# Quantizing tokens and down weights among the scans instead of ahead of them, in a fused state-space and FP4 feed-forward block

## The chip, the cores and the metric

The kernel runs on one core of one Trainium2 chip. The metric is device time in microseconds (us): the median over runs of the whole program. The core has five engines that work side by side, each through its own instructions in order: TensorE (PE; its weight loads are listed as PEld), VectorE (DVE), ScalarE (ACT), GpSimd (POOL) and SyncE (SP), which here issues nearly all transfers between the device's main memory and the on-chip memory (SBUF). Matrix products land in a second on-chip memory, PSUM, which PE, DVE and ACT reach. Engines wait for each other through semaphores.

## What is computed

Input is x of 8 x 1024 tokens of 512 features; the output is x plus two branches that both read the layer-normalized tokens. In short:

```python
xn = (x - mean(x)) / sqrt(var(x) + 1e-5)
# branch 1: selective state-space layer, 1024 inner channels, 16 states
xb, z = split(xn @ W_in)                     # 512 -> 2 x 1024
xc = silu(causal_conv4(xb) + conv_b)
B, C, d = split(xc @ W_x)                    # 16, 16 and 1 column
dt = softplus(d + dt_bias)
h_t = h_{t-1} * exp(dt_t * A) + dt_t * xc_t * B_t      # per channel and state
y = (sum_states(h_t * C_t) + xc * D) * silu(z)
out1 = y @ W_out
# branch 2: feed-forward with FP4 blocks of 16, 1408 inner features
def fp4(v):                                  # per block of 16 along the last axis
    s = max(max(abs(v)) / 6, 1e-12)
    return nearest_of(0, .5, 1, 1.5, 2, 3, 4, 6)(abs(v / s)) * sign(v) * s
g = fp4(xn) @ fp4(w_gate).T;  u = fp4(xn) @ fp4(w_up).T
out2 = fp4(silu(g) * u) @ fp4(w_down).T
out = x + out1 + out2
```

## The kernel before

The 8192 tokens are cut into 16 steps of 512 (two to a sequence); a step is four tiles of 128 tokens. The recurrence runs along time in one DVE instruction, the scan (`scan`, L553). A scan covers 128 rows (32 channels by 4 states) and two stretches of 512 time steps, so 64 scans, called pairs here, make a step, and there are 1,024.

**A pair.** POOL makes `u` (`make_u`, L523, two pairs ahead, three buffers), ACT makes the decays `ah` in PSUM with two exponentials (`make_a`, L535, one pair ahead, two buffers), DVE scans `ah` with `u` and multiplies by C into `hc` (L560, four buffers), PE sums the states into `py` (`sum_states`, L570).

**The preparation.** All that the pairs and the feed-forward read is made first and left in main memory (`run`, L795 to L815): gate and up weights in 12 pieces (`prepare_gate_up`), down weights in 8 (`prepare_down`), tokens in 32 halves of a step (`normalize`). Each piece is quantized (`quantize`: the maximum of each block of 16 at L74, scales, the product with the inverse scale at L81, all on DVE; `step_of`, ACT's absolute value and exponential, which give the rounding step; POOL's sum, difference and product at L83 to L85), then transposed on PE and copied by ACT (`transposed`). A token half is transposed twice, normalized alone (`xnT`, for branch 1) and quantized (`xqT`, for branch 2). Its pool has two buffers of each tile. Step 0's projections and convolution (`ahead`) are woven in, one part after each piece.

**The pairs' stage.** The order is written out by hand (`tc.manual_schedule`), pair by pair, in `sweep`: `make_u`, `make_a`, `scan`, then what fell due (`issue`), then other work by a budget of time per pair. Other work comes from generators that yield their estimated cost: `finish` (the step before: output projection, pairs 2 to 9), `ahead` (the next step: projections, convolution with ACT's `taps` and POOL's sums at L365, from pair 9 on), and `others`: in steps 0 to 9 `gate_up` (gate and up products, silu, quantization of the hidden piece on DVE, ACT and POOL at L671 to L693, transposes L706), in steps 10 to 15 `downs` (L779). `later(n, work)` puts work n pairs ahead; a work that returns `AGAIN` is put off by a pair; `key` keeps an order, and `act` limits ACT's long work in a pair. PE's products outside `py` take one of three PSUM banks (`bank`, `frees`), and a generator is only asked while `room` finds one. After step 9's last pair `gate_up` is run to its end before `downs` starts.

## Time and profile before

| | us |
|---|---|
| median of 3 runs | 5291.96 (5284.35 to 5296.69) |
| the profiled execution: its time | 5304.77 |
| its span, first to last instruction | 5302.8 |
| first scan starts at | 567.6 |
| steps 0 to 9 | 567.6 to 3716.3 |
| steps 10 to 15, and the last projection | 3716.3 to 5302.8 |
| mean granted clock of PE | 0.90 |

Busy time is the time in which an engine had an instruction in work. A page cuts the span in 40 slices of 132.6 us and shows each engine's busy share in tenths. A table by stretches gives busy us and, in brackets, the instructions; then PE's granted clock, the transfer engines' share and GB/s. A wait is shown as who waited for whom: us in total, how often, the longest. In a group of instructions stand line, engine, operation, out<-in, shapes and count, then busy us and the mean ns of one, then the engine's idle time before them and who ended it.

### The profile page before, as it was taken

What the parts mean: (1) busy time and instruction counts of PE and PEld (TensorE: products, weight loads), DVE (VectorE), ACT (ScalarE), POOL (GpSimd) and SP (SyncE); (2) the same over time, 40 slices, a digit from 0 to 9 for tenths busy, and PEclk for the clock granted to TensorE, in tenths of its full rate; (3) what the DMA queues carried; (4) which work ended last, traced back from release to release, by engine and by line L of the source; (5) the groups of instructions that cost most, each with busy time, mean ns of one, the idle gap of its engine ahead of it and who ended that gap; (6) DMA issues with size and microseconds to landing.
All of it is one profiled execution on the core that took longest, in us unless ns stands there. A gap on an engine that the chain in (4) does not pass through costs nothing.

```text
span 5302.8 us, 52505 instructions
## 1 busy us (share of the span) xinstructions
PE 4385.3 (83%) x16324; PEld 2301.2 (43%) x16324; DVE 4498.5 (85%) x4191; ACT 3408.8 (64%) x5089; POOL 4041.0 (76%) x2338
## 2 busy tenths in 40 slices
PE   4433688989889898988988889896999999999975
PEld 2222446455555645555564555652333333333321
DVE  3477688888888889888897888889898999999997
ACT  4655567685767758676675767767465656665543
POOL 6655688887878889887897888878676777777664
PEclk8655799999999999998999999997999999999986
DMA  5555457565575766656565576756677778687852
GB/s 160 159 159 156 134 155 202 160 196 161 159 197 152 204 174 180 182 163 181 168 191 155 168 187 177 204 144 192 173 219 188 219 187 241 172 240 188 233 132 60
DMA packets 625191, 937.48 MB, mean 177 GB/s; under 512 B 54400, under 2 KB 373888, under 8 KB 622736
## 3 DMA queue, kind: packets, MB, share of 16 engines
q1 hardware_dynamic: 614512, 931.61, 63.1%
q10 hardware_dynamic: 10400, 2.52, 0.2%
q8 instruction: 130, 2.13, 0.2%
q14 instruction: 149, 1.22, 0.1%
HBM read 676.76 MB, written 257.20 MB: 176 GB/s over the span
## 4 chain that ended last, share of the span: by engine, by line
PE 26%; DVE 21%; ACT 12%; DMA 5%; issue 4%; POOL 3%; SPq 0%; DVEq 0%; ACTq 0%; POOLq 0%
DVE ah L553 12%; PE po L620 8%; DVE hc L560 6%; PE pu L656 4%; PE pod L779 4%; ACT ah L535 4%; PE pg L656 3%; PE py L570 2%; PE pz L383 2%; PE px L345 2%; DMA rep<-ddd 2%; POOL u L523 1%; DMA xz<-z 1%; ACT L535 1%; ACT taps L359 1%
## 5 line engine op out<-in xcount | busy, mean ns | idle before, releaser
L523 POOL TENSOR_TENSOR u<-rep,B 128x1024 f32<-128x1024 f32 x1024 | 2409.9, 2359 | 755.0 <-DVE ah L553 695.7
L535 ACT ACTIVATE ah<-rep,A 128x512 f32<-128x512 f32 x2048 | 1415.9, 692 | 1139.1 <-DVE hc L560 1102.5
L560 DVE TENSOR_TENSOR hc<-ah,C 128x1024 f32<-128x1024 f32 x1024 | 1248.6, 1219 | 78.2 <-PE py L570 35.5
L553 DVE TENSOR_TENSOR_SCAN ah<-ah,state,u 128x1024 f32<-128x1024 f32 x512 | 1199.1, 2342 | 89.2 <-ACT u L541 88.2
L553 DVE TENSOR_TENSOR_SCAN ah<-ah,u 128x1024 f32<-128x1024 f32 x512 | 1169.4, 2284 | 65.2 <-ACT ah L535 60.4
L570 PE MATMUL py<-hc,summed 128*32 128x512 f32 x4096 | 648.8, 633 | 170.6 <-DVE hc L560 119.8
L656 PE MATMUL pu<-wu,xq 128*128 128x256 f32 (+1 forms) x3072 | 695.7, 384 | 102.5 <-ACT hT L709 63.5
L656 PE MATMUL pg<-wg,xq 128*128 128x256 f32 (+1 forms) x3072 | 662.6, 373 | 71.0 <-ACT hT L709 27.0
L656 PEld LDWEIGHTS pu<-wu,xq 128*128 128x128 f32 x3072 | 573.1, 203 | 252.5 <-ACT hT L709 88.2
L779 PE MATMUL pod<-dT,hTr 128*128 128x512 f32 x1408 | 645.4, 609 | 17.3 <-DMA hTr<-hT 9.2
L656 PEld LDWEIGHTS pg<-wg,xq 128*128 128x128 f32 x3072 | 555.1, 196 | 211.3 <-issue 70.2
L383 PE MATMUL pz<-xT,wz 128*128 128x512 f32 x1024 | 513.2, 648 | 79.7 <-ACT h L667 34.8
L345 PE MATMUL px<-xT,wx 128*128 128x512 f32 x1024 | 491.1, 624 | 38.1 <-ACT h L667 21.4
L365 POOL TENSOR_TENSOR xc<-xc,taps 128x509 f32<-128x509 f32 (+2 forms) x384 | 440.6, 1147 | 52.9 <-ACT taps L359 34.1
L620 PE MATMUL po<-Wout,y 128*128 128x512 f32 x1024 | 466.7, 608 | 12.4 <-ACT hT L709 4.4
L779 PEld LDWEIGHTS pod<-dT,hTr 128*128 128x128 f32 x1408 | 263.8, 193 | 400.3 <-issue 362.0
L383 PEld LDWEIGHTS pz<-xT,wz 128*128 128x128 f32 x1024 | 206.5, 208 | 354.9 <-issue 235.9
L570 PEld LDWEIGHTS py<-hc,summed 128*32 128x32 f32 x4096 | 91.0, 110 | 561.3 <-DVE hc L560 282.7
L345 PEld LDWEIGHTS px<-xT,wx 128*128 128x128 f32 x1024 | 194.7, 198 | 315.5 <-issue 223.4
L620 PEld LDWEIGHTS po<-Wout,y 128*128 128x128 f32 x1024 | 192.2, 193 | 282.2 <-issue 258.9
L671 DVE TENSOR_TENSOR h<-h,pu 128x512 f32<-128x512 f32 x192 | 121.6, 636 | 190.0 <-PE pu L656 176.6
L535 ACT ACT_TABLE_LOAD x209 | 268.1, 1283 | 3.7
(113 smaller groups left out, 4619.5 us busy)
## 6 DMA issues: line engine op xcount, KB each, us to landing
rep<-ddd SPq DMA_DIRECT2D x512, 512.0 KB, 7.1
ddd<-dd SPq DMA_DIRECT2D x128, 512.0 KB, 4.5
hTr<-hT SPq DMA_DIRECT2D x64, 704.0 KB, 6.7
wg<-gu SPq DMA_DIRECT2D x80, 512.0 KB, 4.9
wu<-gu SPq DMA_DIRECT2D x80, 512.0 KB, 5.2
hT<-hT SPq DMA_DIRECT2D x80, 512.0 KB, 3.1
wx<-in_L_attn_W_in_dram SPq DMA_DIRECT2D x128, 256.0 KB, 3.0
wz<-in_L_attn_W_in_dram SPq DMA_DIRECT2D x128, 256.0 KB, 2.9
```

What stands on the lines that cost most here:

```text
L345: nc.tensor.matmul(px, w[:, k, :], s.xT[:, k, :], start=(k == 0), stop=(k == self.KM - 1))
L365: tt(ca[:, H0 - k :], ca[:, H0 - k :], taps[k][:, : T - H0 + k], ALU.add)
L383: nc.tensor.matmul(b[0], w[:, k, :], s.xT[:, k, :], start=(k == 0), stop=(k == self.KM - 1))
L523: self.nc.gpsimd.tensor_tensor(u, s.reps[j][:, h : h + 2, 1, :], s.B[q].unsqueeze(1).to_broadcast([P, 2, T]), ALU.mult)
L535: nc.scalar.activation(ah[:, i, :], s.reps[j][:, h + i, 0, :], AF.Exp, scale=self.A[:, g, q : q + 1])
L553: nc.vector.tensor_tensor_scan(a, a, u.rearrange("p i t -> p (i t)"), 0.0 if s.first else self.state[:, g, q : q + 1], ALU.mult, ALU.add,)
L560: nc.vector.tensor_tensor(hc, ah, s.C[q].unsqueeze(1).to_broadcast([P, 2, T]), ALU.mult)
L570: nc.tensor.matmul(s.py[i * D4 : (i + 1) * D4, :], self.summed, hcs[i // 2][:, i % 2, :], start=(q == 0), stop=(q == NG - 1),)
L620: nc.tensor.matmul(b[0], s.y[:, j, i * P : (i + 1) * P], self.Wout[:, j, :], start=(j == 0), stop=(j == self.J - 1),)
L656: nc.tensor.matmul(b[0][:, i, :], xq[pair][:, k, i * P : (i + 1) * P], w[:, k, :], start=(k == 0), stop=(k == self.KM - 1),)
L671: nc.vector.tensor_tensor(rows, rows, b[0], ALU.mult)
L779: nc.tensor.matmul(b[0], h[:, k, :], dT[:, k, :], start=(k == 0), stop=(k == self.KF - 1))
```

## The change

The preparation keeps the gate and up weights and the tokens of steps 0 to 2 (`FIRST = 3`). The tokens of the other 13 steps (52 tiles of 128 x 512) and the down weights (12 tiles, four of them 384 columns wide) are handled in the pairs' stage, one tile at a time:

- `measure`: in step 0, a token tile a pair is loaded and DVE takes its mean and variance; `norms` then makes all factors at once.
- `tile_later`: the tile is loaded again; ACT normalizes it in place (`normal`) and PE transposes it (`turn`); DVE takes the block maxima, POOL the two scales (`scale`); DVE the reciprocal, POOL the product (`quotient`); ACT absolute value and exponential, POOL sum, difference and product (`round_`); PE transposes again. ACT copies each transpose, SP stores it. Down tiles have no normalization and one transpose.
- `next_tile` starts a tile when the one before has come far enough, in all of step 0 and in pairs 10 to 52 of the others. `turn_tiles` takes free PSUM banks for transposes and counts 0.5 us of the budget for each. `gate_up` waits with the load of a step's tokens until all four tiles are stored.
- In the preparation `quantize` has its last product on DVE with the scale in PSUM, tokens are stored before they are quantized, step 0's quantization comes after four weight pieces, `ahead` takes two parts after each piece, and step 0's convolution runs on DVE from PSUM (`convolve_first`).
- The tiles `r` of residuals come from one pool with four buffers, shared with the new tiles.

Blank lines and unchanged lines are left out.

```diff
@@ -38,6 +38,7 @@
 AGAIN = "again"
+FIRST = 3
 TAIL = 12
@@ -73,8 +74,6 @@
     nc.vector.tensor_scalar(sc, top, 1.0 / 6.0, TINY, ALU.mult, ALU.max)
-    scs = pool.tile([P, n], F32, tag="qs", name=f"qs_{name}")
-    nc.vector.tensor_copy(scs, sc)
     nc.vector.reciprocal(rs, sc)
@@ -82,7 +81,7 @@
     nc.gpsimd.tensor_tensor(v, v, m, ALU.subtract)
-    nc.gpsimd.tensor_tensor(blocks(v), blocks(v), spread(scs, n), ALU.mult)
+    nc.vector.tensor_tensor(blocks(v), blocks(v), spread(sc, n), ALU.mult)
     return v
@@ -181,6 +180,8 @@
             )
+        n = (self.n - FIRST) * self.TT
+        self.norm = cpool.tile([P, n, 2], F32, tag="norm", name="norm")
         self.Win_v = W_in.rearrange("(k p) n -> p k n", p=P)
@@ -216,18 +217,6 @@
-    def prepare_down(self, pp, r, k0):
...
@@ -260,14 +249,170 @@
         flat = xn.rearrange("p i h -> p (i h)")
-        xq = quantize(nc, pp, self.p_a, flat, G * H, self.steep, f"x{name}")
-        for src, dst in ((flat, self.xnT_d), (xq, self.xqT_d)):
+        def put(src, dst):
             st = self.transposed(pp, src, G * self.KM, f"{dst[c].name}_{half}")
...
+        def rest():
+            put(quantize(nc, pp, self.p_a, flat, G * H, self.steep, f"x{name}"), self.xqT_d)
+        put(flat, self.xnT_d)
+        return rest
+    def measure(self, i):
+        nc = self.nc
+        t = (FIRST * self.TT + i) * P
+        x = self.pool.tile([P, self.DM], F32, tag="r", name=f"xm_{i}", bufs=4)
+        nc.sync.dma_start(x, self.x[t : t + P, :])
+        def moments():
+            stats = self.pool.tile([P, 6], F32, tag="stat", name=f"stat_m{i}", bufs=1)
+            nc.vector.bn_stats(stats, x)
+            nc.vector.bn_aggr(self.norm[:, i, :], stats)
+        self.later(2, moments, key="m")
+    def norms(self):
+        nc, n = self.nc, self.norm.shape[1]
+        b = self.pool.tile([P, 3, n], F32, tag="r", name="rstd_m", bufs=4)
+        rstd, err, one = b[:, 0, :], b[:, 1, :], b[:, 2, :]
+        mean, var = self.norm[:, :, 0], self.norm[:, :, 1]
+        tt, ts, stt = nc.vector.tensor_tensor, nc.vector.tensor_scalar, nc.vector.scalar_tensor_tensor
+        nc.scalar.activation(one, var, AF.Sqrt, bias=self.eps)
+        nc.vector.reciprocal(rstd, one)
+        tt(err, rstd, rstd, ALU.mult)
+        stt(err, var, EPS, err, ALU.add, ALU.mult)
+        ts(err, err, -0.5, 1.5, ALU.mult, ALU.add)
+        tt(rstd, rstd, err, ALU.mult)
+        stt(mean, mean, -1.0, rstd, ALU.mult, ALU.mult)
+        nc.vector.tensor_copy(var, rstd)
+    def tile_later(self, name, src, norm, dsts, rounded):
+        nc = self.nc
+        W = src.shape[1]
+        n = W // BLK
+        x = self.pool.tile([P, W], F32, tag="r", name=f"xl_{name}", bufs=4)
+        nc.sync.dma_start(x, src)
+        small = {}
+        def turn(dst, kind, done):
+            b = self.bank([P, W], f"pt{kind}_{name}")
+            for k in range(W // P):
+                nc.tensor.transpose(b[0][:, k * P : (k + 1) * P], x[:, k * P : (k + 1) * P], self.ident)
+            def copy():
+                st = self.pool.tile([P, W // P, P], F32, tag="r", name=f"xs{kind}_{name}", bufs=4)
+                nc.scalar.copy(st, b[0].rearrange("p (k t) -> p k t", t=P))
+                def store():
+                    nc.sync.dma_start(dst, st)
+                    done()
+                self.later(1, store, key="x")
+            self.later(1, copy, [b], "x", 0.6)
+        def normal():
+            nc.scalar.activation(x, x, AF.Identity, bias=norm[:, 0:1], scale=norm[:, 1:2])
+            self.turns.append(lambda: turn(dsts[0], "n", done))
+            self.later(1, scale, key="x")
+        def scale():
+            for k in "tsr":
+                small[k] = self.pool.tile([P, n], F32, tag=f"xl{k}", name=f"xl{k}_{name}", bufs=1)
+            nc.vector.tensor_reduce(small["t"], blocks(x), AX.X, ALU.max, apply_absolute_value=True)
+            nc.gpsimd.tensor_scalar(small["s"], small["t"], 1.0 / 6.0, TINY, ALU.mult, ALU.max)
+            nc.gpsimd.tensor_scalar(small["t"], small["s"], UP, None, ALU.mult)
+            self.later(1, quotient, key="x")
+        def quotient():
+            if self.turns:
+                return AGAIN
+            nc.vector.reciprocal(small["r"], small["t"])
+            nc.gpsimd.tensor_tensor(blocks(x), blocks(x), spread(small["r"], n), ALU.mult)
+            self.later(1, round_, None, "x", 1.5)
+            done()
+        def round_():
+            if self.rounding:
+                return AGAIN
+            m = step_of(nc, self.fp, x, W, self.steep, f"xl_{name}")
+            nc.gpsimd.tensor_tensor(x, x, m, ALU.add)
+            nc.gpsimd.tensor_tensor(x, x, m, ALU.subtract)
+            nc.gpsimd.tensor_tensor(blocks(x), blocks(x), spread(small["s"], n), ALU.mult)
+            self.later(
+                1, lambda: self.turns.append(lambda: turn(dsts[-1], "q", rounded)), None, "x"
+            )
+        self.turning = 1 if norm is None else 2
+        def done():
+            self.turning -= 1
+        if norm is None:
+            self.later(2, scale, None, "x")
+        else:
+            self.later(2, normal, None, "x", 0.8)
+    def tiles(self):
+        n = self.norm.shape[1]
+        for i in range(n):
+            yield lambda i=i: self.measure(i)
+        for _ in range(2):
+            yield lambda: None
+        yield "norms"
+        for i in range(n):
+            c, o = divmod(FIRST * self.TT + i, self.TT)
+            t = (c * self.TT + o) * P
+            def rounded():
+                self.normalized += 1
+            tok = slice(o * P, (o + 1) * P)
+            yield lambda c=c, t=t, tok=tok, i=i, rounded=rounded: self.tile_later(
+                f"x{i}", self.x[t : t + P, :], self.norm[:, i, :],
+                [self.xnT_d[c][:, :, tok], self.xqT_d[c][:, :, tok]], rounded,
+            )
+        for r in range(self.KM):
+            for k0 in range(0, self.KF, 4):
+                kn = min(4, self.KF - k0)
+                rows = slice(r * P, (r + 1) * P)
+                yield lambda r=r, k0=k0, kn=kn, rows=rows: self.tile_later(
+                    f"d{r}_{k0}", self.weights_of[2][rows, k0 * P : (k0 + kn) * P], None,
+                    [self.dT_d[:, k0 : k0 + kn, rows]], lambda: None,
+                )
+    def next_tile(self):
+        if self.turning or self.queue is None:
+            return
+        if self.queued == "norms":
+            self.norms()
+        elif self.queued:
+            self.queued()
+        self.queued = next(self.queue, None)
+        if self.queued is None:
+            self.queue = None
+    def turn_tiles(self):
+        us = 0.0
+        while self.turns and self.room():
+            self.turns.pop(0)()
+            us += 0.5
+        return us
@@ -351,6 +496,10 @@
             )
+            if not self.timed:
+                self.convolve_first(j, ca, px)
+                s.convolved += 1
+                return
             taps = []
@@ -374,6 +523,19 @@
+    def convolve_first(self, j, ca, px):
+        nc, H0 = self.nc, self.H0
+        over = self.over[:, j, :]
+        nc.scalar.activation(over, px[:, T - H0 :], AF.Copy, scale=self.cw[:, j, 0:1])
+        for k in range(H0):
+            w = self.cw[:, j, k : k + 1]
+            to = [(ca[:, H0 - k :], px[:, : T - H0 + k])]
+            if k:
+                to.append((over[:, : H0 - k], px[:, T - H0 + k :]))
+            for o, i in to:
+                nc.vector.scalar_tensor_tensor(o, i, w, o, ALU.mult, ALU.add)
@@ -592,10 +754,10 @@
-    def rest(self, pool, t):
+    def rest(self, t):
         seen = t in self.r_seen
-        r = pool.tile([P, self.DM], F32, tag="r", name=f"r_{t}_{seen}")
+        r = self.pool.tile([P, self.DM], F32, tag="r", name=f"r_{t}_{seen}", bufs=4)
         self.nc.sync.dma_start(r, self.r_d[t] if seen else self.x[t * P : (t + 1) * P, :])
@@ -609,12 +771,12 @@
         nc = self.nc
-        rs = [self.rest(self.pool, s.c * self.TT)]
+        rs = [self.rest(s.c * self.TT)]
         yield 0.0
...
             if i:
-                rs.append(self.rest(self.pool, t))
+                rs.append(self.rest(t))
             b = self.bank([P, self.DM], f"po_{t}")
@@ -687,9 +849,18 @@
             self.later(1, lambda: tt(blocks(v), blocks(flat), spread(rs, blk), ALU.mult), key="g")
-            self.later(2, lambda: m.append(step_of(nc, fp, v, K, self.steep, f"{c}_{n}")), None, "g", 2.1)
+            def begin():
+                self.rounding = True
+                m.append(step_of(nc, fp, v, K, self.steep, f"{c}_{n}"))
+            def end():
+                tt(v, v, m[0], ALU.subtract)
+                self.rounding = False
+            self.later(2, begin, None, "g", 2.1)
             self.later(3, lambda: tt(v, v, m[0], ALU.add), key="g")
-            self.later(4, lambda: tt(v, v, m[0], ALU.subtract), key="g")
+            self.later(4, end, key="g")
             self.later(5, lambda: tt(blocks(v), blocks(v), spread(sc, blk), ALU.mult), key="g")
@@ -747,6 +918,8 @@
                 if n == len(self.pieces) - 1 and i + 1 < len(order):
+                    while self.normalized < self.TT * (order[i + 1][0] + 1):
+                        yield 0.0
                     load_x(order[i + 1][0], pair)
@@ -773,7 +946,7 @@
             h = hs.pop(0)
-            r = self.rest(fp, t)
+            r = self.rest(t)
             b = self.bank([P, self.DM], f"pod_{t}")
@@ -791,35 +964,38 @@
         self.partly = set()
+        self.normalized, self.turning, self.turns, self.rounding = FIRST * self.TT, 0, [], False
+        self.queue, self.queued = self.tiles(), None
         self.us, self.ahs, self.step = [], [], {}
         with tc.tile_pool(name="prep", bufs=2) as pp:
-            for half in range(2):
-                self.normalize(pp, 0, half)
+            quants = [self.normalize(pp, 0, half) for half in range(2)]
             s = self.step[0] = self.begin(0)
...
+            def more(c, h):
+                self.normalize(pp, c, h)()
...
                     for r in range(0, KF, 2) for g in range(2)]
-            work += [lambda r=r, k=k: self.prepare_down(pp, r, k)
-                     for r in range(self.KM) for k in range(0, KF, 8)]
-            work += [lambda c=c, h=h: self.normalize(pp, c, h)
-                     for c in range(1, n) for h in range(2)]
-            for w in work:
+            work[4:4] = quants
+            work += [lambda c=c, h=h: more(c, h) for c in range(1, FIRST) for h in range(2)]
+            for i, w in enumerate(work):
                 w()
-                next(first, None)
-            for _ in first:
-                pass
-            for q in range(NG):
-                self.fetch_bc(s, "B", q)
-                self.fetch_bc(s, "C", q)
-            for i in range(SG):
-                self.fetch(s, 0, i)
+                for _ in range(2):
+                    next(first, None)
+                if i == 9:
+                    for q in range(NG):
+                        self.fetch_bc(s, "B", q)
+                        self.fetch_bc(s, "C", q)
+                    for i in range(SG):
+                        self.fetch(s, 0, i)
         self.timed = True
...
         with ExitStack() as ffn:
-            fp = ffn.enter_context(tc.tile_pool(name="ff", bufs=2))
+            fp = self.fp = ffn.enter_context(tc.tile_pool(name="ff", bufs=2))
             with tc.manual_schedule():
@@ -869,6 +1045,8 @@
             self.fetches(c, k)
+            if c == 0 or QUIET < k < per - 11:
+                self.next_tile()
             if g + 2 < len(pairs):
@@ -890,6 +1068,8 @@
             due = 29.0 * (k - END_Y + 1) / (QUIET - END_Y) if END_Y <= k < QUIET and c else 0.0
+            if not self.hold:
+                left -= self.turn_tiles()
             while left > done - credit or ended < due:
@@ -917,6 +1097,8 @@
         while more:
+            self.next_tile()
+            self.turn_tiles()
             if self.room("other"):
```

## The prediction

> **What bounds the kernel now.** I read the page first, then the busy time by stretches cut at the starts of the scans (L553; the first of 1,024 starts at 567.6 us, and 64 make a step), then who waits in the first ten steps, then the preparation's groups by form.
>
> ```profile
> span 5302.8 us, 52505 instructions
> PE 4385.3 (83%) x16324; PEld 2301.2 (43%) x16324; DVE 4498.5 (85%) x4191; ACT 3408.8 (64%) x5089; POOL 4041.0 (76%) x2338
> DVE  3477688888888889888897888889898999999997
> POOL 6655688887878889887897888878676777777664
> PEclk8655799999999999998999999997999999999986
> ```
>
> No engine is bound over the whole span. The first four or five slices are the preparation: no engine near full, PE at half clock.
>
> ```profile
> core 0: us, PE busy (x) PEld busy (x) DVE busy (x) ACT busy (x) POOL busy (x), PEclk, DMA share, GB/s
> 0.00:200.00 200.00, 93.86 (x262) 49.23 (x262) 69.28 (x153) 102.74 (x138) 130.38 (x106) 0.82 0.50 150
> 200.00:567.60 367.60, 129.36 (x506) 94.90 (x506) 274.86 (x518) 219.92 (x285) 208.53 (x112) 0.53 0.52 159
> ...
> 567.60:910.70 343.10, 279.88 (x1238) 182.36 (x1239) 271.40 (x274) 222.76 (x305) 273.85 (x150) 0.91 0.59 162
> 910.70:3425.20 2514.50, 2219.33 (x9368) 1352.25 (x9367) 2161.43 (x1921) 1773.28 (x2618) 2101.36 (x1216) 0.94 0.64 177
> 3425.20:3716.30 291.10, 227.51 (x840) 107.92 (x840) 253.79 (x180) 202.24 (x329) 234.75 (x144) 0.84 0.61 175
> 3716.30:5014.90 1298.60, 1232.81 (x3583) 454.57 (x3582) 1222.40 (x990) 777.32 (x1207) 947.33 (x552) 0.98 0.75 205
> ```
>
> These are: the weights' share of the preparation, its token share, step 0, steps 1 to 8, step 9, steps 10 to 14. Steps 10 to 14 take 1298.6/5 = 259.7 us each with DVE 94% busy: DVE bounds them. Steps 1 to 8 take 2514.5/8 = 314.3 us with PE 88%, DVE 86%, POOL 84%, ACT 71%: no single bound, but engines that wait for each other.
>
> ```profile
> DVE h L671 <- PE pu L656: 176.6, 77, 25.3
> DVE ah L553 <- ACT u L541: 76.4, 49, 11.8
> DVE ah L553 <- POOL u L523: 3.9, 3, 1.8
> POOL u L523 <- DVE ah L553: 295.2, 206, 27.1
> ```
>
> In steps 0 to 9 DVE idles mostly for PE and ACT, almost never for POOL, which itself sits 295.2 us waiting for scans to give back a buffer of `u`. That 295.2 us is POOL's slack.
>
> **What leaves the preparation.** 26 of 32 halves of tokens, all 8 pieces of the down weights; two multiplications move from POOL to DVE (L85, and the taps of step 0), and `ahead` advances twice per piece instead of once. What is left: 10 weight pieces of 1024 columns, 2 of 512, 6 token halves. The rows:
>
> ```profile
> L83 POOL TENSOR_TENSOR qv_x<-qv_x,qm_x 128x1024 f32<-128x1024 f32 x31 | 65.9, 2124 | 174.7 <-ACT qm_x L62 166.8 <-DVE qp_x L74 7.9
> L81 DVE TENSOR_TENSOR qv_x<-xn,qp_x 128x1024 f32<-128x1024 f32 x32 | 39.0, 1219 | 2.5
> L254 DVE TENSOR_SCALAR err<-err 128x2 f32<-128x2 f32 x32 | 28.1, 880 | 0.7
> ```
>
> DVE per full piece: maximum 1.22, two small 0.23, reciprocal 0.56, product 1.22, and the new last product, which like L81 has its scale in PSUM, 1.22: 4.7 us, so 16 x 4.7 + 2 x 2.6 = 80. A token half adds two moments (0.68 + 0.17 each), two normalizations (0.76 each) and about 2.9 of small steps: 6 x 6.1 = 37. Step 0's taps: 8 x 3 at 0.75 (row L588, same form) and small ones, 21. DVE in all: 138 us. POOL falls to 16 x 4.25 + 2 x 2.3 + 8 x 1.27 + three `u` at 2.34 = 90, ACT to about 100 plus 23 table loads of 1.28 = 128 (67 loads before), PE to 109. DVE is now the engine with most to do. At the 75% (274.86/367.6) that it reached in the token stretch, 138 us need 184; by pace, 24 us to the first quantization, 13 pieces at 8 (8.7 before, when POOL had 1.93 more per piece and the taps), 4 halves at 12.7 (11.7 before plus 1.2, less overlap) give 179, and some 8 for the last product, 187. First scan at 190 instead of 567.6: **-378**. Bounds: DVE 90% busy, 153 + 15 = 168; DVE at the whole preparation's 61% (344.14/567.6), 226.
>
> **What goes into the steps.** The order of the changed program shows 52 moments in step 0, token tiles 1, 8, 8, 7, 7, 7, 7, 7 in steps 0 to 7, and the 12 down tiles in steps 8 and 9. Per tile of 512 columns:
> - POOL: products 1.06 and 1.06, sum and difference 1.16 each (rows L689 to L693 at 128x512), two steps on 128x32 for which no POOL row exists (0.19 for L371 on 128x2; 0.85 for L85 on 384 columns), taken 0.2 as 32 columns are nearest the small one: 4.84. 60 tiles at 4.84 and 4 of 384 columns at 3.9: 306.
> - DVE: maximum 0.695 and reciprocal 0.357 (rows L680, L685 at 512 columns), 63 + 3; moments 52 x 0.85 = 44; the eight short `norms` 2: 112.
> - ACT: normalization 0.69 (taken as L359, which reads PSUM), copies 0.58 (116 of them), absolute value 0.63 and exponential 0.72: 188, plus 2.6 for the square root's table in step 0. Absolute value, identity and copies add no table load: 352 stand in the first ten steps before, 352 in the changed order.
> - PE: 116 groups of transposes at 0.61 (four at 0.153, row L706): 71.
>
> Sum 306 + 112 + 191 + 71 = 680 us of engine time. What that costs is read from the steps themselves: steps 10 to 14 hold (1232.81 + 1222.40 + 777.32 + 947.33)/5 = 836 us of work and take 259.7; steps 1 to 8 hold (2219.33 + 2161.43 + 1773.28 + 2101.36)/8 = 1032 and take 314.3. That is 54.6/196 = 0.28 us per us of added work: 680 x 0.28 = **+190**. Bounds: 0, if all lands in POOL's 295.2 and the other engines' gaps; 306, if POOL's work adds one for one.
>
> **The end of step 9.** Before, the last gate and up product ends at 3624.7 us, in pair 40 of step 9's 64. The tiles take PSUM banks and turns, so in the changed order they run on through step 9, and after its last scan 1.5 pieces still pass: DVE scales, POOL 1.94, ACT 2.2, POOL 6.2, then the half piece, POOL 1.06, ACT 1.34, POOL 3.4, with `u` of the third pair behind them on POOL. Some 25 us in series; DVE needs two prepared scans of it (7): **+20**, bounds 5 and 30.
>
> **New waits.** POOL's sum follows the exponential in the same turn (in `gate_up` it is one turn later), PE's transpose follows ACT's normalization in the same turn, and DVE's reciprocal waits for POOL's 0.2 us steps with the next scan behind it on DVE. 64 tiles; the nearest row is DVE's wait for `pu`, 176.6/77 = 2.3 us. Ends 0 and 64 x 2.3 = 147; since POOL is now ahead of the scans (206 of 640 `u` waited for one), I take **+30**. SyncE gets 232 transfers of 256 KB more, 59 MB or 19 GB/s over 3149 us; steps 10 to 14 carry 205 against 177 here, and a store waits for a copy of the turn before, with the next `rep` behind it. POOL waited only 6.4 us for `rep`, so 0; were that cover gone it would show there and is inside the 147.
>
> One rule speaks against the change. The Trainium skill, SBUF — State Buffer, "Who interferes with whom", says that VectorE and GpSimd share a port pair under an exclusive lock. The trace shows such blocking: L254, on 128x2, took 880 ns in the mean beside busy POOL, L249 on the same size 158. By the rule only instructions with two SBUF inputs or in a two-port mode contend, and the tiles' maxima do not. Were all 180 of the tiles' DVE steps held half a POOL instruction (0.55), the sum would be 99 us higher.
>
> **Sum.** 5302.8 - 378 + 190 + 20 + 30 = 5165 of span. The profiled execution took 5304.8, 2.0 more than its span and 0.24% over the median of 5292.0; so 5167, and 5155 on the median's scale.
>
> **Rivals.**
> 1. Slower. POOL becomes the bound at one place: DVE's reciprocal waits for POOL in every tile, so POOL's 306 and the 147 both come on top: -378 + 453 = +75, 5367. It decides from 378/64 = 5.9 us per tile. For it: POOL 84% busy with 12% more work, steps 1 to 8 hold 51 token tiles and 10 down tiles, 294, and by the order 22 POOL steps of `gate_up` less at 2.03, so 2101 + 294 - 45 = 2350 of 2514, 93%. Against: POOL's 295.2 of waiting for scans, and DVE's 3.9 of waiting for `u`.
> 2. Hidden. POOL's slack takes the tiles; only the end of step 9 and 40 in step 0 (DVE 271 + 44 of 343) remain: 5302.8 - 378 + 60 = 4985. Against: DVE, PE and ACT get 374 us too.
> 3. The preparation stays a chain (maximum, ACT, POOL, DVE, PE, two buffers deep) and ends at 250: 5225. For it: POOL waited 166.8 us for ACT there.
> 4. The tiles are not where the change says: excluded by the order, 1%.
>
> **How the numbers follow.** Likeliest 62% (5155, own range 5080 to 5250), slower 9%, hidden 13%, long preparation 15%. Range: hidden side cut at 5020, the slower case's edge at 5285, leaving some 8% on each side. Within 0.2% (about 10 us, what a measurement of this kernel can tell from no change) falls 3%, from the passage between the cases; slower 10%; faster 87%.
>
> **What would show it.** First scan near 190; steps 1 to 7 at 325 to 345 us with POOL at 88 to 92%; step 0 at 360 to 385; step 9 near 350; steps 10 to 15 unchanged within 1%. Wrong if POOL passes 95% in steps 1 to 7, if DVE waits over 100 us for POOL, or if the first scan is after 230.

## The result, and the profile after

| | before | after |
|---|---|---|
| median | 5288.3 us (4 runs) | 5352.25 us (4 runs, 5340.3 to 5366.94) |
| ratio | | 1.0122, 95% interval 1.0097 to 1.0147 |
| profiled span | 5302.8 | 5365.2 |

The changed kernel is 1.2% slower. The prediction was 5155 us, faster. The head of the page of the changed kernel:

```profile
span 5365.2 us, 52431 instructions
...
PE 4404.6 (82%) x16324; PEld 2312.5 (43%) x16324; DVE 4378.0 (82%) x3980; ACT 3379.2 (63%) x5117; POOL 4094.3 (76%) x2554
...
DVE  6489867878878788787787778778698999999997
...
POOL 4387788788887888888878799778576777777654
PEclk9588988988989899899898898999899999999986
```

All busy times are nearly those of before; only the places differ. The two or three weak slices at the head are gone, and in their place DVE's row shows 7s and 8s up to slice 28 where it showed 8s and 9s. The same by stretches, cut at the starts of the scans (preparation, step 0, steps 1 to 8, step 9, step 10):

```profile
core 0: us, PE busy (x) PEld busy (x) DVE busy (x) ACT busy (x) POOL busy (x), PEclk, DMA share, GB/s
0.00:224.40 224.40, 98.39 (x320) 52.54 (x320) 119.62 (x221) 120.19 (x157) 90.17 (x53) 0.79 0.64 191
224.40:592.00 367.60, 289.14 (x1214) 185.49 (x1214) 314.93 (x386) 224.85 (x305) 267.96 (x150) 0.89 0.70 187
592.00:3380.50 2788.50, 2262.31 (x9338) 1360.40 (x9337) 2197.57 (x2004) 1894.70 (x2849) 2352.00 (x1560) 0.90 0.61 172
3380.50:3738.40 357.90, 309.19 (x1286) 190.31 (x1285) 275.52 (x217) 242.16 (x377) 277.03 (x171) 0.92 0.59 163
3738.40:4039.30 300.90, 254.60 (x757) 98.98 (x756) 246.59 (x230) 155.34 (x223) 202.10 (x113) 0.92 0.68 186
```

Against before: preparation -343.2, step 0 +24.6, steps 1 to 8 +274.0, step 9 +66.8, step 10 +38.3, the rest +1.9: together +62. In steps 1 to 8 POOL has 251 us more, ACT 121, PE 43, DVE 36. No engine passes 85% there, so none became the bound, and yet 451 us of added work cost 274 us. Nor is POOL the bound in the pairs that hold the tiles: in pairs 10 to 57 steps 1 to 7 grew by 212 of their 241 us (from 1639.8 to 1852.0), and POOL was 86% busy there, against 85% before. The waits in steps 0 to 9 (first DVE's, then POOL's, then PE's) say who stood still:

```profile
DVE h L833 <- PE pu L818: 251.2, 96, 8.1
DVE ah L715 <- ACT u L703: 124.4, 74, 11.9
DVE ah L715 <- ACT ah L697: 73.6, 37, 8.0
...
DVE xlr_x L343 <- POOL xlt_x L337: 38.1, 8, 6.4
...
POOL u L685 <- DVE ah L715: 252.1, 130, 18.7
POOL xls_x L336 <- DVE xlt_x L335: 60.9, 24, 8.4
...
POOL xl_x L352 <- ACT qm_xl_x L63: 47.4, 26, 4.4
...
PE ptn_x L313 <- ACT xl_x L328: 65.5, 18, 9.0
...
PE ptq_x L313 <- POOL xl_x L354: 38.4, 12, 8.2
```

Before, the scans' second wait for ACT was

```profile
DVE ah L553 <- ACT ah L535: 48.3, 34, 4.6
```

So the scans wait longer for ACT (76.4 + 48.3 became 124.4 + 73.6), DVE's product `h`, with the scans behind it, waits longer for PE (176.6 became 251.2), and a row of new waits names the tiles' own instructions (`xl`, `pt`): each engine waits for the step that another makes of the same tile. The experiments ask how much of the 404 us of steps 0 to 10 is due to what.

### The profile page after: what moved, and what is told of

It reads as the page before. It is cut to its first block, busy times and chain, and to the rows that moved or that the text cites. A ratio compares the mean times of both kernels' runs of the same rounds, so it can differ in the third digit from the quotient of the medians.

```text
span 5365.2 us, 52431 instructions
## 1 busy us (share of the span) xinstructions
PE 4404.6 (82%) x16324; PEld 2312.5 (43%) x16324; DVE 4378.0 (82%) x3980; ACT 3379.2 (63%) x5117; POOL 4094.3 (76%) x2554
## 4 chain that ended last, share of the span: by engine, by line
PE 33%; DVE 23%; ACT 16%; POOL 12%; DMA 9%; issue 5%; SPq 1%; ACTq 0%; DVEq 0%; POOLq 0%
DVE ah L715 12%; PE po L782 9%; PE pu L818 7%; DVE hc L722 6%; PE pod L952 4%; ACT ah L697 4%; PE pz L545 3%; POOL u L685 3%; PE px L490 3%; PE py L732 3%; PE pg L818 2%; DMA rep<-ddd 2%; DMA xz<-z 2%; POOL xc L514 2%; ACT L697 1%
## 5 line engine op out<-in xcount | busy, mean ns | idle before, releaser
L818 PE MATMUL pu<-wu,xq 128*128 128x256 f32 (+1 forms) x3072 | 730.4, 399 | 97.6 <-ACT hT L880 26.2
L732 PE MATMUL py<-hc,summed 128*32 128x512 f32 x4096 | 637.3, 635 | 138.1 <-DVE hc L722 98.3
L818 PEld LDWEIGHTS pu<-wu,xq 128*128 128x128 f32 x3072 | 601.4, 213 | 252.1 <-ACT hT L880 38.7
L514 POOL TENSOR_TENSOR xc<-xc,taps 128x509 f32<-128x509 f32 x360 | 413.5, 1149 | 36.8 <-ACT taps L508 17.8
L833 DVE TENSOR_TENSOR h<-h,pu 128x512 f32<-128x512 f32 x192 | 121.9, 637 | 281.3 <-PE pu L818 251.2
```

What stands on the lines that cost most here:

```text
L514: tt(ca[:, H0 - k :], ca[:, H0 - k :], taps[k][:, : T - H0 + k], ALU.add)
L732: nc.tensor.matmul(s.py[i * D4 : (i + 1) * D4, :], self.summed, hcs[i // 2][:, i % 2, :], start=(q == 0), stop=(q == NG - 1),)
L818: nc.tensor.matmul(b[0][:, i, :], xq[pair][:, k, i * P : (i + 1) * P], w[:, k, :], start=(k == 0), stop=(k == self.KM - 1),)
L833: nc.vector.tensor_tensor(rows, rows, b[0], ALU.mult)
```

## The experiments

All lengths are differences of scan starts in each run's trace (scans 1, 65, 577, 641, 705). The last column but one is what steps 0 to 10 took more than the 3411.2 us of before. Each row is one profiled execution. Those of before and after took 16 and 15 us more than their medians, the others at most 9 more or 5 less; so a difference of less than some 20 us is not told by two rows alone, and where it matters the medians stand beside it.

| run | first scan | step 0 | 1 to 8 | 9 | 10 | 0 to 10 | span |
|---|---|---|---|---|---|---|---|
| before | 567.6 | 343.0 | 2514.5 | 291.1 | 262.6 | 0 | 5302.8 |
| after | 224.4 | 367.6 | 2788.5 | 357.9 | 300.9 | +404 | 5365.2 |
| xfer | 224.6 | 355.4 | 2525.9 | 324.3 | 304.8 | +99 | 5055.9 |
| dve_alone | 224.4 | 360.7 | 2516.8 | 290.9 | 265.9 | +23 | 4979.3 |
| pool_alone | 224.3 | 356.5 | 2564.5 | 299.4 | 265.9 | +75 | 5029.2 |
| act_alone | 224.5 | 361.3 | 2573.5 | 290.6 | 263.6 | +78 | 5034.2 |
| np_apart | 225.6 | 357.2 | 2685.5 | 317.8 | 270.8 | +220 | 5175.5 |
| no_pe | 223.8 | 353.3 | 2757.5 | 310.2 | 263.3 | +273 | 5230.1 |
| bank_only | 226.6 | 363.3 | 2760.4 | 357.7 | 302.5 | +373 | 5335.4 |
| no_pool | 225.1 | 360.9 | 2698.9 | 351.7 | 301.8 | +302 | 5260.3 |
| apart | 225.6 | 369.6 | 2748.1 | 369.1 | 320.9 | +396 | 5355.2 |
| paid | 226.2 | 359.5 | 2791.2 | 345.2 | 273.6 | +358 | 5317.3 |
| late_fetch | 215.0 | 352.5 | 2774.1 | 356.7 | 301.6 | +374 | 5323.7 |
| paid_late | 215.1 | 349.8 | 2793.7 | 343.7 | 272.2 | +348 | 5296.4 |
| p120l | 215.8 | 352.3 | 2835.6 | 339.3 | 262.6 | +379 | 5330.5 |
| p120lds | 214.9 | 353.2 | 2828.4 | 346.3 | 265.4 | +382 | 5333.5 |
| all3 | 213.6 | 352.1 | 2755.8 | 374.8 | 288.1 | +360 | 5308.8 |
| down_prep | 270.9 | 369.9 | 2751.8 | 339.6 | 291.9 | +342 | 5349.0 |
| f10_30 | 335.1 | 360.4 | 2656.8 | 320.8 | 269.0 | +196 | 5258.7 |
| f10_30s | 334.3 | 358.0 | 2670.8 | 320.8 | 270.8 | +209 | 5282.5 |

### First four: the same turn, POOL, PE's banks, the fetches

**apart**: each step of a tile at least one pair behind the one that feeds it. The two small steps and the reciprocal go to DVE in one turn, POOL's sums come a pair after the exponential, the transposes a pair after their input.

```diff
-            self.turns.append(lambda: turn(dsts[0], "n", done))
+            self.later(1, lambda: self.turns.append(lambda: turn(dsts[0], "n", done)), key="x")
-            nc.gpsimd.tensor_scalar(small["s"], small["t"], 1.0 / 6.0, TINY, ALU.mult, ALU.max)
-            nc.gpsimd.tensor_scalar(small["t"], small["s"], UP, None, ALU.mult)
+            nc.vector.tensor_scalar(small["s"], small["t"], 1.0 / 6.0, TINY, ALU.mult, ALU.max)
+            nc.vector.tensor_scalar(small["t"], small["s"], UP, None, ALU.mult)
+            nc.vector.reciprocal(small["r"], small["t"])
...
             m = step_of(nc, self.fp, x, W, self.steep, f"xl_{name}")
+            self.later(1, lambda: sums(m), None, "x")
+        def sums(m):
             nc.gpsimd.tensor_tensor(x, x, m, ALU.add)
```

> The change with every step of a tile at least one pair behind the engine that feeds it: transposes one pair after ACT's normalization and two after POOL's last product, both small scales and the reciprocal on DVE in one pair, POOL's sums one pair after the exponential. Same work but 26 us of small steps moved from POOL to DVE. Theory W (engines stand in order behind one another in the same turn): steps 1 to 8 fall from 348.6 us each to 325 or less, the whole to about 5150 to 5200. Theory P (POOL's 306 us add one for one because the pairs' chain leaves no room): steps 1 to 8 stay within 5 us of 348.6, the whole within 40 us of 5352. Theory B (three PSUM banks and PE's turns are what is short): also little change, and step 9 gets longer, since by the order 424 gate and up products instead of 360 now fall into it.

Measured: median 5352.7, ratio 1.0122 (1.0099 to 1.0145), as slow as the change. But the stages moved: steps 1 to 8 lost 40 us, steps 9 and 10 took 31 of it back, since by the recorded order 56 gate and up products (40 in the change) were left after the last scan of step 9. Steps 1 to 8 at 343.5 us each miss theory W's 325; little change and a longer step 9 (369.1 against 357.9) is what theory B said, and theory P's figures are nearly met too. So the same-turn waits were not the whole price, and this run could not price them: it also put the small steps on DVE, which turned out dear (below).

**no_pool**: of POOL's four passes over a tile three are left out (sum, difference, last product), so the tile is not rounded.

```diff
-            nc.gpsimd.tensor_tensor(x, x, m, ALU.add)
-            nc.gpsimd.tensor_tensor(x, x, m, ALU.subtract)
-            nc.gpsimd.tensor_tensor(blocks(x), blocks(x), spread(small["s"], n), ALU.mult)
+            nc.gpsimd.tensor_tensor(x[:, :16], x[:, :16], m[:, :16], ALU.add)
```

> The change without POOL's sum, difference and last product on the tiles (16 columns of one sum are left), so tokens and down weights are not rounded: 64 x 3.4 = 215 us of POOL's work less, the order of everything else the same. P: the first ten steps get about 200 us shorter, the whole about 5150. W: only the 53 us of POOL's waits for the exponential and 38 of PE's waits for POOL go, at most 100 us. B: under 50 us.

Measured: 5262.7, ratio 0.9947 (0.9927 to 0.9966). 215 us of POOL out gave 102 us in steps 0 to 10 (90 by the medians). POOL's work, with the waits around it, costs about half its length here, neither nothing nor all: theory P falls, POOL is not the bound.

**no_pe**: no transposes, no PSUM bank, no budget for turns; ACT copies the tile itself, which is stored untransposed.

```diff
-            b = self.bank([P, W], f"pt{kind}_{name}")
-            for k in range(W // P):
-                nc.tensor.transpose(b[0][:, k * P : (k + 1) * P], x[:, k * P : (k + 1) * P], self.ident)
...
-                nc.scalar.copy(st, b[0].rearrange("p (k t) -> p k t", t=P))
+                nc.scalar.copy(st, x.rearrange("p (k t) -> p k t", t=P))
...
-            self.later(1, copy, [b], "x", 0.6)
+            copy()
```

> The change without the tiles' 116 groups of transposes: ACT copies the tile itself, PE and the PSUM banks are left to the rest, and the stored tiles are not transposed. PE has 71 us less work; 170 us of PE's idle time in steps 1 to 8 stood before these transposes. B, and the part of W that is PE's: steps 1 to 8 fall by 20 us or more each, and step 9 by some 40, as by the order 184 gate and up products instead of 360 fall into it and none after its last scan; the whole about 5100. P: steps 1 to 8 fall by less than 8 us each, only the end of step 9 gains.

Measured: 5236.44, ratio 0.9897 (0.9877 to 0.9917): 71 us of PE gone give 131 in steps 0 to 10, and 85 of those lie in steps 9 and 10, where few tiles are. By the order no product is left after step 9, against 40 in the change. Steps 1 to 8 fell by 3.9 us each, not by theory B's 20: the gain is at the end of step 9. Theory P had said this, but its reason, POOL as the bound, falls with no_pool.

**late_fetch**: step 0's fetches of B, C and `rep` are issued after the last piece of the preparation instead of after the tenth.

```diff
-                if i == 9:
+                if i == len(work) - 1:
```

> The change with step 0's loads of B, C and rep issued after the last piece of the preparation instead of after the tenth. Theory S (SyncE stood in order behind the chain from x_proj over dt to rep, so that the stores of weights and the loads of tokens behind it came late; DVE busy 3.5 of 25 us between 150 and 175): first scan at 185 to 200 us instead of 224.4, the whole 25 to 40 us shorter, nothing else moved. Rival (the chain of a piece is what is slow): first scan within 8 us of 224, or later, as rep now lands after it.

Measured: 5329.72, ratio 1.0075 (1.0059 to 1.0092), 23 us less than after. The first scan comes 9 us earlier (theory S had said 24 to 39) and step 0 is 15 shorter. In the change SyncE issues, from 131 to 173 us, nothing but these fetches and the stores of `dd` that `rep` is read from, which wait for POOL to make it (19.9 us in all); the stores and loads of the next pieces stand behind them. The next load of tokens goes out at 177.9 us, with the late fetches at 136.1. The stretch from 150 to 175 us, first in the changed kernel:

```profile
150.00:175.00 25.00, 0.39 (x2) 0.00 (x0) 3.50 (x6) 8.72 (x9) 9.17 (x6) 0.50 0.48 167
```

and with the late fetches:

```profile
150.00:175.00 25.00, 7.80 (x32) 5.66 (x30) 17.62 (x44) 17.33 (x22) 13.42 (x8) 0.50 0.61 204
```

DVE worked 3.5 of 25 us in the one and 17.6 in the other. DVE's wait for a load of tokens fell from 28.4 to 8.6 us.

### Transfers, banks, the budget, the down weights

**xfer**: a tile is loaded and stored at its places, nothing else.

```diff
-            self.later(2, normal, None, "x", 0.8)
+        self.later(4, store, None, "x")
```

> Leaves out all arithmetic on the tiles: each tile is loaded, stored untransposed at its one or two places, and not normalized, rounded or turned (moments and norms stay). Same bytes and the same 232 transfers on SyncE. Theory W (what the tiles cost is their arithmetic on POOL, ACT, PE and DVE): preparation -343, step 0 about +20 for the moments, steps 1 to 8 as before within 10 us each, step 9 and 10 near before plus 25 because gate and up products still end later by the order (pair 57 of step 9 instead of 40): span near 5005, at most 5040. Theory T (the transfers and SyncE's queue carry a good part of the +274 of steps 1 to 8): 5080 or more, with steps 1 to 8 at 325 us or more each.

Measured: 5055.99 (2 runs), ratio 0.9547. Steps 1 to 8 take 2525.9 us against 2514.5: the 232 transfers and SyncE's queue cost some 11 us, no more than two rows can tell apart, and theory T falls. Steps 9 and 10 are 75 longer, which neither theory had: here a tile is held for seven pairs, tokens come late and so do the products that wait for them (the last starts in pair 57 of step 9, before in pair 40). In dve_alone, which holds a tile for six pairs and has the same transfers, it is pair 40 again and steps 9 and 10 are as before.

**bank_only**: no transposes, but each group claims its bank and its 0.5 us of budget, and ACT's copy stands where it stood.

```diff
             b = self.bank([P, W], f"pt{kind}_{name}")
-            for k in range(W // P):
-                nc.tensor.transpose(b[0][:, k * P : (k + 1) * P], x[:, k * P : (k + 1) * P], self.ident)
-                nc.scalar.copy(st, b[0].rearrange("p (k t) -> p k t", t=P))
+                nc.scalar.copy(st, x.rearrange("p (k t) -> p k t", t=P))
```

> Leaves out the 4 transposes of each of the 116 groups, but each group still claims a PSUM bank for its pair, pays 0.5 us of the planner's budget and its copy by ACT stands where it stood (from the tile itself): the order of all other work is that of the changed kernel, with 40 gate and up products after the last scan of step 9. Theory Q (what the transposes cost is that they push gate and up products back, through the bank and the budget): span 5310 to 5365, so far above the 5230 that the kernel without transposes and without their banks took. Theory M (PE's 71 us and its waits for ACT and POOL in the same turn cost by themselves): 5230 to 5280.

Measured: 5335.82, ratio 1.0075 (1.0049 to 1.0102), as theory Q said. Neither this nor no_pe has the transposes. They differ in the claims, the budget for them, and the place of ACT's copy: a pair after the claim here, in the same turn in no_pe. Steps 1 to 8, 9 and 10 of bank_only:

```profile
589.90:3350.30 2760.40, 2203.14 (x8889) 1307.98 (x8890) 2194.70 (x2003) 1897.61 (x2850) 2353.91 (x1563) 0.90 0.63 173
3350.30:3708.00 357.70, 308.37 (x1282) 190.37 (x1281) 275.52 (x217) 242.14 (x377) 277.02 (x171) 0.93 0.59 164
3708.00:4010.50 302.50, 257.19 (x769) 99.69 (x768) 246.69 (x231) 155.28 (x223) 202.07 (x113) 0.93 0.69 187
```

and of no_pe:

```profile
577.10:3334.60 2757.50, 2264.06 (x9300) 1370.21 (x9296) 2214.14 (x2041) 1943.91 (x2903) 2404.61 (x1593) 0.91 0.64 177
3334.60:3644.80 310.20, 244.70 (x912) 124.13 (x912) 257.35 (x185) 209.41 (x339) 244.47 (x151) 0.84 0.62 173
3644.80:3908.10 263.30, 246.49 (x711) 91.48 (x710) 244.53 (x224) 146.31 (x211) 187.62 (x104) 0.96 0.73 195
```

Same length in steps 1 to 8, but no_pe did 411 more PE instructions there, which bank_only does in steps 9 and 10, 87 us longer. So the claims, with the later copy, cost 100 us (373 - 273; 99 by the medians), the transposes themselves 31 (404 - 373; 16 by the medians). The drain is seen in DVE's waits of the changed kernel after step 9's last scan: the first `downs` product waits for the last hidden piece.

```profile
DVE r_False L769 <- PE pod L952: 35.3, 1, 35.3
```

**paid**: the planner's total for the gate and up sweep holds what the turns take out of it.

```diff
-        costs = [sum(14.4 * w / FB + 0.6 * (w // P) for _, w in self.pieces) * n, ...
+        costs = [sum(14.4 * w / FB + 0.6 * (w // P) for _, w in self.pieces) * n + 58.0, ...
```

> One number: the planner's total for the gate and up sweep is raised by 58 us (116 groups at 0.5), which is what the turns take out of it. By the order no gate or up product is left after the last scan of step 9, and the last comes in pair 55. Theory Q (gate and up products are late because the turns are paid from their budget, and the end of step 9 is a drain): the drain of about 38 us at the head of step 10 goes and step 9 falls a little: span 5290 to 5325. Theory M (the same work is only moved to earlier steps, which are as full): step 10 loses 38 and steps 1 to 8 gain about as much: 5345 to 5375.

Measured: 5313.17, ratio 1.0036 (1.0024 to 1.0048). Step 10 loses 27 us, step 9 13, steps 1 to 8 stay: theory Q.

**down_prep**: the down weights are back in the preparation, 8 pieces.

```diff
+            work += [lambda r=r, k=k: self.prepare_down(pp, r, k)
+                     for r in range(self.KM) for k in range(0, KF, 8)]
```

> Undoes one part: the down weights are quantized in the preparation again, in 8 pieces of 1024 columns or less; tokens stay in the scans. First scan later by 8 pieces at 8 to 8.7 us: 288 to 294 instead of 224. Steps 8 and 9 lose 12 tiles, and 8 instead of 40 products are left after the last scan. Theory Q (late gate and up products): steps 8 to 10 fall by 60 to 110 together, as the drain is nearly gone: span 5325 to 5375, about as after. Theory M (0.6 us per us of a tile's 9 us on the engines, 12 tiles): steps 8 to 10 fall by 65: 5365 to 5375. If steps 8 to 10 fall by under 40: slower than after, over 5385.

Measured: 5351.89, ratio 1.0105 (1.0087 to 1.0123). Steps 0 to 10 fall by 62, or 5.2 per tile; the preparation grows by 46.5, not 64 to 70. By the medians, which are equal, the steps gave back just those 46.5, or 3.9 per tile. Undoing this part changes nothing that the runs can tell.

### Each engine's work by itself, and three edits together

In pool_alone, dve_alone and act_alone, as in xfer, the tile's other arithmetic is left out. In these three the gate and up products stand, by the order, where they stood before the change.

```diff
+        def work():                                       # pool_alone
+            for op in (ALU.mult, ALU.add, ALU.subtract, ALU.mult):
+                nc.gpsimd.tensor_tensor(x, x, x, op)
+        def work():                                       # dve_alone
+            nc.vector.tensor_reduce(t, blocks(x), AX.X, ALU.max, apply_absolute_value=True)
+            self.later(1, lambda: nc.vector.reciprocal(r, t), None, "x")
+        def work():                                       # act_alone
+                nc.scalar.activation(x, x, AF.Identity, bias=norm[:, 0:1], scale=norm[:, 1:2])
+                self.later(1, lambda: copied(dsts[0], done), None, "x")
+            self.later(2, round_, None, "x")
```

pool_alone, act_alone and dve_alone, in this order:

> As the run with transfers alone (steps 1 to 8: 2526 us), plus four POOL passes over each tile, all in one turn, two turns after its data should be there, waiting for nobody but the load. 57 tiles of 64 lie in steps 1 to 8: about 250 us of POOL. Gate and up products stand as in the kernel before. Theory L (POOL's slack takes most of it, 0.28 us per us as predicted): steps 1 to 8 at 2596, within 25. Theory R (POOL's work costs what leaving a part of it out gave back, 0.42 to 0.5 per us): 2630 to 2655. One for one: 2770.

> As the run with transfers alone, plus ACT's work on each tile: normalization, absolute value, exponential and a copy per store (the tile itself is copied; no maxima, no POOL, no transposes). About 62 tiles lie in steps 1 to 8: some 180 us of ACT. Theory L (0.28 per us): steps 1 to 8 at 2526 + 50 = 2576, within 25. Theory R (ACT's work delays the exponentials of the next scan and what PE waits for): 0.5 or more per us, 2615 or more.

> As the run with transfers alone, plus the maximum and the reciprocal on DVE for each tile, 57 of them in steps 1 to 8, some 60 us. Theory L (0.28 per us): steps 1 to 8 at 2543, within 10. Theory R (DVE, which every scan waits for, takes it one for one): 2580 to 2595. With the two runs beside it: if the three additions sum to 210 or more, the tiles cost the sum of their parts; if to 150 or less, some 100 us come from the order in which one tile's work goes through the engines.

Measured: 5034.86, 5034.03 and 4983.5, ratios 0.9516, 0.9515, 0.9419. Steps 1 to 8 of pool_alone, act_alone and dve_alone:

```profile
580.80:3145.30 2564.50, 2233.56 (x9369) 1362.68 (x9367) 2163.95 (x1920) 1775.51 (x2618) 2334.10 (x1446) 0.94 0.69 190
```

```profile
585.80:3159.30 2573.50, 2221.79 (x9369) 1352.28 (x9367) 2165.21 (x1921) 1940.63 (x2909) 2104.06 (x1216) 0.94 0.69 191
```

```profile
585.10:3101.90 2516.80, 2219.29 (x9380) 1351.90 (x9372) 2205.63 (x2034) 1773.58 (x2618) 2100.75 (x1216) 0.95 0.70 194
```

Against the 2514.5 of before: POOL's 232.7 us more (2334.1 - 2101.4) cost 50.0, 0.21 per us; ACT's 167.4 cost 59.0, 0.35 per us; DVE's 44.2 cost 2.3. Theory R falls for all three. ACT's steps lie in theory L's range; POOL's and DVE's came out below it, by 6.5 and 16 us. The sum is 111 of the 274, so the larger part of the price is not the work of one engine by itself. Over steps 0 to 10 DVE's work takes 23, POOL's 75 and ACT's 78; the 23 of DVE holds the moments of step 0, which the other two have too (step 0 is 12 to 18 longer in xfer and these three). With 16 of each taken as that common part, 16 + 7 + 59 + 62 = 144, to some 20 us.

**all3** is late_fetch, paid and apart in one.

> The changed kernel with three edits together: the fetches for the first scan issued after the last piece of the preparation, the turns added to the planner's total, and each step of a tile at least one pair behind the one that feeds it. By the order no product is left after step 9, the last in pair 59. If they add up (about -30, -40 and, in steps 1 to 8, -40): span 5240 to 5280, faster than before by up to 1%. If the gain in steps 1 to 8 is again given back in steps 9 and 10, as it was without the planner's total: 5285 to 5310, no better than before.

Measured: 5310.67, ratio 1.0037 (1.0023 to 1.0050): the gain of steps 1 to 8 was given back in steps 9 and 10 again (375 and 288).

### What is left: hand-overs, the budget again

**np_apart** is no_pe and apart together.

> Without the transposes and their PSUM banks (the tile is stored untransposed), and each step of a tile at least one pair behind the one that feeds it, with the small steps on DVE. All other arithmetic of the tiles stays. The parts measured alone predict steps 1 to 8 at 2515 + 2 + 50 + 59 = 2626, about 2635 with the small steps on DVE. Theory S (the rest is waits of one step for another in the same turn): 2626 to 2670, span 5080 to 5130. Theory E (the engines' work costs more when all of it is there, since each engine then has less slack to take the others' delays): 2700 or more, span 5170 or more.

Measured: 5172.91, ratio 0.9775 (0.9753 to 0.9797); steps 1 to 8 at 2685.5, between the two theories. Without the banks in the way, keeping the steps a pair apart gives 53 us (273 - 220; 64 by the medians); with them it gave 8 (404 - 396). Part of what holds np_apart above the 144 of the parts can be the small steps on DVE. DVE's groups of np_apart:

```profile
L335 DVE TENSOR_SCALAR xls_x<-xlt_x 128x32 f32<-128x32 f32 x51 | 62.0, 1215 | 29.4 <-POOL xl_x L357 26.5
L336 DVE TENSOR_SCALAR xlt_x<-xls_x 128x32 f32<-128x32 f32 x51 | 58.5, 1148 | 1.8
L334 DVE TENSOR_REDUCE xlt_x<-xl_x 128x32 f32<-128x512 f32 x51 | 34.4, 675 | 0.1
L337 DVE RECIPROCAL xlr_x<-xlt_x 128x32 f32<-128x32 f32 x51 | 18.0, 353 | 1.8
```

The same steps on POOL in the changed kernel, and in the kernel before on DVE with one operand in PSUM (`pu`):

```profile
L336 POOL TENSOR_SCALAR xls_x<-xlt_x 128x32 f32<-128x32 f32 x52 | 16.9, 324 | 63.4 <-DVE xlt_x L335 60.9
L337 POOL TENSOR_SCALAR xlt_x<-xls_x 128x32 f32<-128x32 f32 x52 | 15.2, 293 | 4.3
```

```profile
L683 DVE TENSOR_SCALAR pu<-sc 128x32 f32<-128x32 f32 x14 | 2.7, 195 | 0.5
L682 DVE TENSOR_SCALAR sc<-pu 128x32 f32<-128x32 f32 x14 | 2.7, 191 | 0.7
```

From SBUF to SBUF beside a busy POOL the step takes 1.15 to 1.22 us on DVE in the mean, six times as long as with PSUM (a single one 0.18 to 2.32; one `u` of POOL takes 2.36); in apart and np_apart that adds about 100 us to DVE. A kernel apart with the scales in PSUM was not run, so how much of the 76 us between 144 and 220 is this, and how much that three engines have less slack at once, stays open.

One more rival no run separates. PE's granted clock in steps 1 to 8 was 0.94 before and 0.94 to 0.95 with one engine's work, 0.92 in np_apart, 0.91 in no_pe, 0.90 in bank_only and the change, and the same products took longer there (`pu` of 256 columns 405 ns before, 416 in no_pe, 418 in the change). By the busy time per product of each form that is, as an estimate, 47 us of PE in np_apart, 55 in no_pe and 69 in the change. PE is 81% busy in steps 1 to 8 of the change, so not all of it need reach the span; whether the lower clock made the steps longer or came of what made them longer stays open.

**p120l** and **p120lds**: late fetches and +120 us instead of +58, so that the products end in pair 42 of step 9; p120lds also has the small steps and the reciprocal on DVE.

p120l, then p120lds:

> The changed kernel with the planner's total raised by 120 us instead of 58 and the fetches for the first scan after the last piece of the preparation. By the order gate and up products stand in steps 1 to 8 as many as before (2544 against 2536), and the last in pair 42 of step 9. Theory Q (the end of the sweep is where the late products cost): step 9 near 310 and step 10 near 265 instead of 358 and 301, steps 1 to 8 at 2790 to 2830: span 5235 to 5285, faster than before by 0.3 to 1.2%. Theory M (moved work costs the same where it goes): steps 1 to 8 at 2860 or more, span 5300 to 5325.

> As the run with the total raised by 120 us and the fetches late, and the tile's two small steps and the reciprocal on DVE behind the maximum, so that POOL no longer waits for the maximum and DVE no longer for POOL. Theory S: the waits POOL for DVE's maximum (61 us in steps 0 to 9) and DVE for POOL (44 us) go, DVE gets 64 times 0.4: 20 to 50 us faster than the run beside it. Theory E: within 15 us of it.

Measured: 5327.37, ratio 1.0063 (1.0049 to 1.0078), and 5332.27, 1.0076 (1.0062 to 1.0091). Against late_fetch, steps 9 and 10 lose 56 us and steps 1 to 8 gain 62. Neither range of p120l was met (2835.6 in steps 1 to 8, a span of 5330.5), but theory M is nearer: products pushed forward cost as much there as they save at the end, and theory Q was only right for the drain. And exchanging DVE's wait for POOL against dear steps on DVE gains nothing.

### The price of a tile, and a version that beats both

paid_late, f10_30 and f10_30s, in this order:

> The changed kernel with the planner's total raised by 58 us and the fetches for the first scan issued after the last piece of the preparation. If the two add up (-37 and -30 us): 5275 to 5295, within 0.3% of before. If not: 5300 to 5330, as with a total raised by 120 us.

> Tokens of 10 of the 16 steps stay in the preparation (14 halves more than in the changed kernel, at 11.7 us: first scan near 379), so that 24 token tiles and the 12 down tiles lie among the scans, the token tiles as close as before, in steps 1 to 4; the total raised by 30 us for their turns, the fetches late. Theory N (a price of about 5.8 us per tile, whatever their number): steps 0 to 10 cost 36 x 5.8 = 209: span 5285 to 5325. Theory V (the price falls with the number, to 3 us or less): span 5180 to 5240.

> As the run beside it, but in steps 1 to 9 a tile begins only in every ninth pair, so that the token tiles spread over steps 1 to 7. Theory N: as the run beside it within 15 us. Theory V: faster than it by 20 us or more, since the tiles of one step no longer follow each other through the same queues; 5170 to 5230.

```diff
-FIRST = 3
+FIRST = 10
-            if c == 0 or QUIET < k < per - 11:            # f10_30s
+            if c == 0 or QUIET < k < per - 11 and g % 9 == 0:
```

paid_late is paid and late_fetch in one; the other two have the late fetches and +30 us. Measured: paid_late 5297.48, ratio 1.0015 (1.0006 to 1.0024): the two edits nearly add up, and all but 8 us of the loss is gone. f10_30 5265.6, ratio 0.9960 (0.9947 to 0.9973): faster than before. f10_30s 5275.64, ratio 0.9976 (0.9965 to 0.9987). Spreading the tiles does not help.

A tile costs 348/64 = 5.4 us in paid_late and 196/36 = 5.4 in f10_30, spread or not near that (209/36 = 5.8): theory N, a price per tile. Its span of 5285 to 5325 was missed all the same (5258.7), because the other side was cheaper than thought. Between paid_late and f10_30, 14 halves more in the preparation moved the first scan from 215.1 to 335.1, 8.6 us each, not the 11.7 of the kernel before. The preparation of f10_30:

```profile
0.00:335.10 335.10, 155.00 (x539) 95.23 (x540) 241.19 (x458) 209.30 (x274) 145.38 (x79) 0.67 0.64 191
```

POOL is 43% busy and DVE 72%; before the change it was 60% (338.91/567.6) and 61%. The product that went from POOL to DVE, and what else the change did to the preparation, made a half 3.1 us cheaper, and a down piece takes 46.5/8 = 5.8 (the expectation of down_prep had 8 to 8.7).

## Why the prediction was wrong

By the profiled spans the change came out 200 us above the prediction's 5165. The work by itself came out 15 us under its term (144 and 31 for the transposes, against 190); 35 us are the preparation's, 99 the new waits' (129 against 30) and 80 the end of step 9's, with its banks (100 against 20). By its own steps:

- **Preparation, -378**: measured -343.2. The bounds held, the size did not: 9 us lie in the fetches that stood in SyncE's queue (late_fetch), and DVE, with 120 us of work instead of 138, was 53% busy (119.62/224.4), not 75%. But the step missed what mattered for the choice: it booked the whole of it as the gain of moving work. At the new price the 26 halves and the down weights would take 26 x 8.6 + 46.5 = 270 us. The other 73 come from the edits to the preparation and need no tile in the scans.
- **What goes into the steps, +190 at 0.28 per us**: the slope was right for what it describes. POOL's work alone cost 0.21, ACT's 0.35, DVE's 0.05 per us, together 144 us over steps 0 to 10. The slope came from steps that hold more or less of the same independent work, and says nothing about work that goes from engine to engine.
- **New waits, +30 (0 to 147)**: this is the step that failed most. The waits were named rightly (POOL for ACT's exponential, PE for ACT's normalization, DVE for POOL's small steps; all three stand in the rows of after) but priced by one row, and "POOL is now ahead of the scans" was taken as cover. Measured: no_pe, without transposes and claims, takes 129 us more than the parts alone (273 - 144), near the step's upper end of 147. 53 of them go when no step follows another in the same turn (np_apart, in spite of its dear small steps); the other 76 come when all the tiles' work is there, and why stays open.
- **The end of step 9, +20**: this step failed too. The drain alone shows 35.3, and the banks and the budget behind it cost 100 (bank_only against no_pe). The prediction saw from the order that the products run on through step 9, and priced only their tail, not that they are 8 to 56 fewer in each of steps 1 to 8 and so 208 more in step 9. The transposes themselves cost 31.
- **SyncE, 0** in the steps: right (dve_alone, +2 in steps 1 to 8). **What would show it**: step 0 and step 9 came as said (367.6, 357.9), steps 1 to 7 at 337 to 370 instead of 325 to 345, POOL at 84%, not 88 to 92, and step 10 was 38 us longer, so steps 10 to 15 grew by 2.5%, not under 1%. None of the three signs of being wrong came (POOL past 95%, DVE over 100 us behind POOL, a first scan after 230), though the time was far off: none of them stood for what failed.
- The ledger of the 404 us: 144 work, 76 all of it together (with the dear small steps of that run), 53 same-turn waits, 100 banks and budget, 31 transposes. The prediction had 240 for it. The ledger follows one order of taking things away, with some 20 us on each entry; in another order the entries differ (the same-turn waits were worth 8 with the banks in place), and the lower clock of PE is spread over them.
- **Rival 1**, at 5367, gave nearly the time, but not by its mechanism: POOL had the work that it named (2352.0 us in steps 1 to 8, named 2350) but 2788 us for it, and did not become the bound; DVE's reciprocal waited 44 us, not for every tile. So the nearness is luck. Its breaking point, 5.9 us per tile, was the useful number (343.2/64 = 5.4 with the preparation as it came): measured 404/64 = 6.3. Rivals 2 and 3 are sums of spans, 10 us above the scale of the median; nothing rests on it.
- **The rule weighed in it** (the Trainium skill, SBUF — State Buffer, "Who interferes with whom"): the 99 us were rightly left out. The tiles' maxima took 676 ns in the change and the reciprocals 345, no more than the rows of before (695 and 357); with 233 us more of POOL in pool_alone, DVE's busy time in steps 1 to 8 stayed at 2164 (2161 before). The rule's other half, that a `tensor_scalar` from SBUF to SBUF can be blocked for a whole instruction of POOL, is what the 1.2 us of np_apart, up to 2.32, agree with.
